# Attention's mask products: features in two 32-bit parts instead of three bfloat16 parts, masks in 32 bits

## The chip, the cores and the metric

The kernel runs on one core of one Trainium2 chip. The metric is the device time of one execution in microseconds; times of several executions are given by their median. The core's engines are called PE (TensorE), DVE (VectorE), ACT (ScalarE), POOL (GpSimd) and SP (SyncE, which issues most DMAs); PEld is PE's loading of weights.

## The reference

Four graph layers run one after the other on x (4096 nodes, 64 features) and one dense matrix adj (4096 x 4096, float32); each ends in a residual sum and a layer norm. Layer 0 is a Chebyshev filter (three products with adj), layer 2 a product with weights that decay along each row's non-zeros, layer 3 a hyperbolic aggregation over all pairs of nodes. The change is in layer 1:

```python
A_node = node_adj - jnp.diag(d_node)          # both are adj
node_support = concat([(A_node > 0) @ h, (A_node < 0) @ h], axis=1)
edge_output = gru_cell(node_support, h, w_ih_e, w_hh_e, b_ih_e, b_hh_e)
hw = h @ W
h_plus, h_minus = (A > 0) @ hw, (A < 0) @ hw
e_plus  = leaky_relu(concat([h_plus, h_minus]) @ a)
e_minus = leaky_relu(concat([h_minus, h_plus]) @ a)
att = softmax(where(A > 0, e_plus, where(A < 0, e_minus, -9e15)), axis=1)
edge_support = (att * A) @ hw
node_output = gru_cell(edge_support, h, w_ih_n, w_hh_n, b_ih_n, b_hh_n)
out = d_edge[:, None] * edge_output + d_node[:, None] * node_output
```

The score of a row does not depend on the column, so all that is needed of adj is the product of the positive (and negative) mask with h, the number of entries, and the product of adj itself with h. Here adj has no negative entry, and the kernel takes at run time the branch that has the positive mask alone (`signed` is false).

## The kernel before

**Stages.** The matrix is cut into 8 x 8 chunks of 512 x 512 floats (1 MB), held as 128 partitions x 4 blocks x 512. The first stage (to some 380 us) loads each chunk, turns it on PE, stores the turned one as `adj_t` and begins the Chebyshev filter; two further passes over parts of `adj_t` end it at about 568 us. Attention (568 to 841 us), the decay layer (to some 1150 us) and the hyperbolic layer follow. The order of the work is written out in Python loops, with steps of earlier rows put between the chunks; a scheduler then sets each engine's order by it, where `in_order` does not fix it.

**Attention.** The function `attention` goes through 64 chunks: rows g from 7 down to 0, in each the chunks c from 0 to 7. For a chunk, `masks` loads it (`load1`, L476, four tiles `at` of 1 MB), makes the mask `pos` (`positives`, L481, on DVE: 1 where the entry is over 0, in fp8, five tiles), and stores this mask for the decay layer (`keep_mask`, L778, issued by POOL). On the diagonal chunk (c = g) the diagonal is then set to zero (L1028), and `pos` is made a second time. `masks` runs two chunks ahead (`lead = 2`). Of the first three chunks, loaded early, `pos` is made before the branch.

PE then has three groups for a chunk, each over its four blocks of 128 rows, with 512 columns:

- `wide` (L1045): the mask with `sp_two`, the high and the middle bfloat16 part of the features side by side, 128 columns of weights;
- `narrow` (L1053): the mask with `sp_lo`, the low bfloat16 part, 64 columns, in two halves of the array by turns;
- `weighed` (L1062): adj itself with the features in float32, 64 columns, in two halves of the array by turns.

An even chunk has them in this order, an odd one in the opposite order, and chunk 7 has `narrow`, `wide`, `weighed`. The parts come from `split` (L244 to L248, five DVE operations for 512 nodes), called in `normed_third` behind layer 0's norm, seven times in the last pass over `adj_t` and once at the start of attention. The last column of the features is replaced: 1 in `sp_hi`, 0 in the others, so that the products also count the entries.

**A row's end and the steps put between.** After chunk 7 ACT copies the sums out of PSUM (`p_t` L1107, `a_t` L1110), and `group_end` gives six steps, one behind each of the next row's chunks. Behind chunk 0: the edge gates on PE (L840, L847), two tanh on ACT (`rz`, L856, with a table load ahead), DVE work, a tanh (`n`, L884), the scores and their exponentials on ACT (L911, L912), the `share` on DVE (L930). Behind chunk 1: a product with `a_t` (L937), its scaling by `share` on ACT (`gin`, L946), and the first half of the node gates (L840), which take the PSUM tile that `gin` has read. Behind chunk 2: the node's tanh (`rz` L874, `n` L884), the second half of the node gates, and the layer norm (a second table load and `ln_s`, L269), whose result is `nat_b`. Behind chunks 4 and 5: three bfloat16 parts of `nat_b` for the decay layer, and copies of them to other partitions, issued by POOL (`over_two`, `over_lo`, L988). In DVE's queue the `pos` of chunk 5 stands behind this layer norm. SP's queue holds the chunk loads and, in rows 7 to 4, reads of stored masks among them (L789 to L792).

Other tiles that the change moves: `part` (layer 0), `nat_b` and `nat_c` (later layers) have tiles of their own; `tr_o` lies in `sp_two`.

Of the kernel before, what the change touches and what calls it, by code (L numbers as in the profile page):

```python
# [8 lines left out]

F32 = mybir.dt.float32  # L10
BF16 = mybir.dt.bfloat16
U16 = mybir.dt.uint16
# [49 lines left out]
def gnn4_kernel(  # L62
# [21 lines left out]
    nc = tc.nc  # L84
# [85 lines left out]

    sp_two = keep.tile([P, NB, 2 * F], BF16, name="sp_two")
    sp_hi = sp_two[:, :, 0:F]
    sp_mid = sp_two[:, :, F : 2 * F]
    sp_lo = keep.tile([P, NB, F], BF16, name="sp_lo")

# [13 lines left out]
    def constant_fills():  # L189
        nc.gpsimd.memset(tr_a[F:P, :], 0.0)  # L190
        nc.gpsimd.memset(sp_hi[:, :, F - 1], 1.0)
        nc.gpsimd.memset(sp_mid[:, :, F - 1], 0.0)
        nc.gpsimd.memset(sp_lo[:, :, F - 1], 0.0)
        nc.gpsimd.memset(none_t, 0.0)
# [283 lines left out]

    def positives(pool, at, **more):
        pos = pool.tile([P, CB, GW], MASK, name="pos", **more)  # L480
        in_order(nc.vector.tensor_scalar(pos, at, 0.0, None, ALU.is_gt, saturate=False))  # L481
        return pos
# [26 lines left out]
    with tc.tile_pool(name="acc", bufs=1) as acc_p, tc.tile_pool(  # L509
# [212 lines left out]
        for g in reversed(range(NG - 1)):  # L722
# [42 lines left out]
    nat_c = three.tile([P, NB, F], F32, name="nat_c")  # L765

    tr_c = tr_x
    tr_o = sp_two[:, 0 : NB // 2, :]  # L770
    nat_b = three.tile([P, NB, F], F32, name="nat_b")
    middle = ctx.enter_context(ExitStack())
# [236 lines left out]
    def attention(signed, cols_p, sg, tl, ps_a, ps_p):  # L1009

        Q = 2 if signed else 1

        def masks(g, c):
            if g == NG - 1 and c < len(with_at):
                at, pos = with_at[c], with_pos[c] if c < len(with_pos) else None
            else:
                at, pos = load1(cols_p, g, c), None
            if not signed and pos is None:
                pos = positives(sg, at)
            mask = pos  # L1020
            if signed:
                mask = sg.tile([P, CB, GW], MASK, name="mask")
                in_order(nc.vector.tensor_scalar(mask, at, 0.0, None, ALU.not_equal, saturate=False))
            keep_mask(mask, g, c)
            if c == g:

                for k in range(CB):
                    in_order(nc.vector.tensor_tensor(at[:, k, cols(k)], at[:, k, cols(k)], not_ident, ALU.mult))  # L1028
                pos = None
            if pos is None:  # L1030
                pos = positives(sg, at)
            if not signed:
                return (pos,), (at,)
            neg = sg.tile([P, CB, GW], MASK, name="neg")
            up = sg.tile([P, CB, GW], F32, name="up")
            in_order(nc.vector.tensor_scalar(neg, at, 0.0, None, ALU.is_lt, saturate=False))
            nc.scalar.activation(up, at, AF.Relu)
# [3 lines left out]
        def wide(ps, two, c):  # L1041
            for k in range(CB):
                jb = c * CB + k
                for q in range(Q):
                    in_order(nc.tensor.matmul(  # L1045
                        ps[q], lhsT=sp_two[:, jb, :], rhs=two[q][:, k, :], start=(jb == 0), stop=(jb == NB - 1)
                    ))

        def narrow(ps, two, c):

            for q in range(Q):
                for k in range(CB):
                    in_order(nc.tensor.matmul(  # L1053
                        ps[q][k % 2 * F : k % 2 * F + F, :], lhsT=sp_lo[:, c * CB + k, :], rhs=two[q][:, k, :],
                        start=False, stop=False, skip_group_check=True,
                    ))

        def weighed(ps, parts, c):

            for k in range(CB):  # L1060
                for q in range(2) if signed else (k % 2,):
                    in_order(nc.tensor.matmul(  # L1062
                        ps[q * F : (q + 1) * F, :], lhsT=nat_a[:, c * CB + k, 0:F],
                        rhs=parts[q if signed else 0][:, k, :],
                        start=(c == 0 and k < 3 - Q), stop=(c == NCH - 1 and k >= CB - 3 + Q), skip_group_check=True,
# [10 lines left out]
        lead = 0 if signed else 2  # L1076
        ahead = [masks(*order[n]) for n in range(lead)]
        steps = [nothing, nothing, lambda ps_p: put_ones(last_row), lambda ps_p: turn_pairs(ps_p, last_row)]
        for n, (g, c) in enumerate(order):
            if n == 0:  # L1080
                normed_third(last_row, sum_last[mine(last_row), :], ps_p)
            if n + lead < len(order):
                ahead.append(masks(*order[n + lead]))
# [3 lines left out]
            two, parts = ahead.pop(0)  # L1087
# [29 lines left out]
    for signed in (False, True):  # L1117
        with cmp.Else() if signed else tc.If(all_positive > 0) as block:
            cmp = block
            with tc.tile_pool(name="cols1", bufs=4 if not signed else 2) as cols_p, tc.tile_pool(name="sign1", bufs=1 if signed else 5) as sg, tc.tile_pool(  # L1120
                name="tail1", bufs=1
# [5 lines left out]
    front.close()  # L1127


    inside = const.tile([P, NB], F32, name="inside")  # L1130
# [600 lines left out]
```

## Time and profile before

| what | us |
|---|---|
| median of three executions | 1499.1 |
| lowest and highest | 1495.8 and 1501.7 |
| span of the profiled execution (first to last instruction) | 1490.4 |
| PE busy | 1355.1 (91%) |
| DVE busy | 1026.1 (69%) |
| ACT busy | 753.2 (51%) |
| POOL busy | 122.7 (8%) |

For the profiled execution the profile gives the span alone; what lies around it is seen only in the distance of 8.7 us between the span and the median of the executions.

A row of the groups reads: line, engine, operation, output<-inputs by the program's names, shapes and types, number; then busy time in us and the mean of one in ns; then the idle time of the engine ahead of it and what ended that. Matmuls overlap and their ends are modelled, so the distance from start to start says what one costs. A float32 product appears as two records. In the order of time a line gives start, time taken, engine, line, operation, number, and in brackets the idle time ahead of it.

### The profile page before, as it was taken

To read this page: it belongs to the slowest core of one execution; us is meant where nothing else is said; L and a number is where in the kernel's file an instruction comes from. 1 tells how busy PE (TensorE), PEld (TensorE's weight loads), DVE (VectorE), ACT (ScalarE), POOL (GpSimd) and SP (SyncE) were. 2 spreads that over 40 slices of the span, in tenths; PEclk is the share of its full clock that TensorE was granted. 3 is DMA by queue.
4 is the path that set the end of the run, shared out by engine and by line. 5 is a ranking of instruction groups with operands and counts; after the bars stand their busy time and mean duration, and the time that the engine had idled before them with its cause. 6 is when DMAs were issued, how large, how long until landed. Compare 5 with 4: busy or idle time off the path is not lost.

```text
span 1490.4 us, 19538 instructions
## 1 busy us (share of the span) xinstructions
PE 1355.1 (91%) x7124; PEld 609.0 (41%) x7124; DVE 1026.1 (69%) x2004; ACT 753.2 (51%) x1303; POOL 122.7 (8%) x206
## 2 busy tenths in 40 slices
PE   5999999999999989889999899999788899889884
PEld 3555555565344323333333332333333334334343
DVE  5989998886000467666677422435899999999995
ACT  3554444342000110222222277564789999999993
POOL 4101100000000002222222100000000000000000
PEclk8999999999999999999999999999899999999996
DMA  9999999997588799788988555552534453544430
GB/s 290 413 410 410 411 410 402 388 359 306 202 281 294 299 419 344 288 307 314 333 328 324 199 176 173 164 168 93 198 141 170 153 216 144 206 165 173 149 113 11
DMA packets 103362, 385.40 MB, mean 259 GB/s; under 512 B 16341, under 2 KB 17369, under 8 KB 71257
## 3 DMA queue, kind: packets, MB, share of 16 engines
q1 hardware_dynamic: 84256, 296.78, 55.2%
q0 software_dynamic: 15616, 85.73, 14.0%
q10 hardware_dynamic: 3384, 1.56, 0.4%
q8 instruction: 58, 0.95, 0.3%
q14 instruction: 48, 0.39, 0.1%
HBM read 297.26 MB, written 85.20 MB: 257 GB/s over the span
## 4 chain that ended last, share of the span: by engine, by line
PE 51%; DVE 20%; ACT 16%; issue 6%; DMA 5%; ACTq 1%; POOL 0%; SPq 0%; DVEq 0%; POOLq 0%
PE tp L637 7%; PE pass L545 7%; PE w_ps L545 7%; PE cnt_ps L1319 4%; PE acc_ps L1275 4%; PE pass L538 3%; PE h_ps L538 3%; PE post L556 2%; DVE at_m L1486 2%; ACT w L1637 2%; DMA at<-adj_t 2%; DVE f L1647 2%; ACT w L1448 2%; ACT rt L1638 2%; ACT wt L1324 2%
## 5 line engine op out<-in xcount | busy, mean ns | idle before, releaser
L644 ACT COPY at<-tp 128x512 f32<-128x512 f32 x256 | 132.6, 598 | 132.2 <-issue 91.9
L1324 ACT ACTIVATE wt<-cnt_ps 128x512 uint16<-128x512 f32 x208 | 115.6, 595 | 70.6 <-PE cnt_ps L1319 65.7
L637 PE MATMUL tp<-ident,raw 128*128 128x128 f32 x1024 | 133.1, 284 | 14.6 <-DMA raw<-in_adj_dram 9.9
L670 DVE TENSOR_REDUCE dpart<-raw 128x4 f32<-128x2048 f32 x64 | 145.4, 2272 | 0.5 <-DMA raw<-in_adj_dram 0.4
L672 DVE TENSOR_REDUCE lows<-raw 128x1 f32<-128x2048 f32 x64 | 145.3, 2271 | 0.0
L1500 PE MATMUL sums_ps<-at_d,nat_c 128*64 128x512 f32 x288 | 140.6, 607 | 2.4 <-DVE at_d L1479 1.8
L637 PEld LDWEIGHTS tp<-ident,raw 128*128 128x128 f32 x1024 | 116.5, 144 | 53.8 <-issue 30.9
L1062 PE MATMUL a_ps<-at,nat_a 128*64 128x512 f32 x512 | 122.4, 605 | 2.9 <-DVE at L1028 2.9
L481 DVE TENSOR_SCALAR pos<-at 128x2048 fp8e4<-128x2048 f32 x72 | 87.6, 1231 | 48.4 <-DMA at<-adj_t 47.9
L1512 PE MATMUL sums_ps<-at_m,nat_c 128*64 128x512 f32 x224 | 107.3, 600 | 0.0
L545 PE MATMUL w_ps<-at,cheb_n 128*128 128x512 f32 x224 | 101.1, 595 | 0.0
L545 PE MATMUL pass<-at,cheb_n 128*128 128x512 f32 x224 | 100.0, 604 | 0.7 <-DVE cheb_n L698 0.7
L1439 PE MATMUL v_ps<-rv,tr_a 64*128 64x512 f32 (+1 forms) x288 | 79.4, 629 | 22.6 <-DVE rt L1662 22.4
L1319 PE MATMUL cnt_ps<-m,follow 128*64 128x512 fp8e4 x480 | 81.7, 391 | 4.6 <-ACT wt L1324 2.1
L1662 DVE SCALAR_TENSOR_TENSOR rt<-v_ps,rt 128x1024 f32<-128x1024 f32 x72 | 83.1, 1154 | 3.7 <-ACT rt L1638 3.4
L1647 DVE SCALAR_TENSOR_TENSOR f<-rt,w 128x1024 f32<-128x1024 f32 x72 | 82.6, 1154 | 2.2 <-ACT rt L1673 2.1
L1650 DVE TENSOR_TENSOR at_d<-at_d,f 128x1024 f32<-128x1024 f32 x72 | 82.9, 1151 | 0.1
L1326 DVE TENSOR_SCALAR wt<-cnt_ps 128x512 uint16<-128x512 f32 x48 | 33.2, 692 | 66.6 <-PE cnt_ps L1319 66.6
L1673 ACT ACTIVATE rt<-rt 128x1024 f32<-128x1024 f32 x72 | 72.4, 1005 | 9.5 <-DVE rt L1662 9.2
L1486 DVE TENSOR_TENSOR at_m<-post,at_m 128x512 f32<-128x512 f32 x112 | 74.4, 678 | 4.0 <-PE post L1484 3.9
L1484 PE MATMUL post<-ident,f 128*128 128x128 f32 x448 | 69.6, 285 | 7.4 <-DVE at_m L1486 6.4
L1637 ACT ACTIVATE w<-w 128x1024 f32<-128x1024 f32 x72 | 72.0, 1002 | 5.0 <-DVE w L1466 5.0
(394 smaller groups left out, 2214.4 us busy)
## 6 DMA issues: line engine op xcount, KB each, us to landing
at<-adj_t SPq DMA_DIRECT2D x122, 1024.0 KB, 6.8
raw<-in_adj_dram SPq DMA_DIRECT2D x64, 1024.0 KB, 12.9
adj_t<-at POOLq DMA_DIRECT2D x64, 1024.0 KB, 8.0
at_d<-adj_t SPq DMA_DIRECT2D x36, 1024.0 KB, 4.7
at_m<-adj_t SPq DMA_DIRECT2D x28, 1024.0 KB, 6.9
mask_t<-pos POOLq DMA_DIRECT2D x64, 256.0 KB, 5.7
m<-mask_t SPq DMA_DIRECT2D x120, 128.0 KB, 2.8
m<-mask_t SPq DMA_DIRECT2D x60, 256.0 KB, 3.8
```

Of the source, the lines that this page charges most:

```text
L545: in_order(nc.tensor.matmul(ps, lhsT=cheb_n[:, jb, k : k + 2, :], rhs=rhs, start=first, stop=last))
L637: in_order(nc.tensor.transpose(tp[:, cols(b)], raw[:, b, cols(k)], ident))
L644: nc.scalar.copy(at[:, k, :], tp)
L670: in_order(nc.vector.tensor_reduce(dpart[:, g, c, :], raw, AX.X, ALU.add))
L672: in_order(nc.vector.tensor_reduce(lows[:, n : n + 1], raw.rearrange("p b j -> p (b j)"), AX.X, ALU.min))
L1062: in_order(nc.tensor.matmul(ps[q * F : (q + 1) * F, :], lhsT=nat_a[:, c * CB + k, 0:F], rhs=parts[q if signed else 0][:, k, :], start=(c = ...
L1319: in_order(nc.tensor.matmul(cnt[a][r * HP : (r + 1) * HP, :], lhsT=follow, rhs=chunks[c][odd][2 * a + r][:, k, :], start=(h == 2 * NB - 1) ...
L1324: in_order(nc.scalar.activation(wt[odd][a], cnt[a], AF.Relu, scale=-128.0))
L1486: work.append(lambda to=to, tp=tp: nc.vector.tensor_tensor(to, tp, to, ALU.mult))
L1500: in_order(nc.tensor.matmul(bank[0:F, :], lhsT=nat_c[:, j * CB + k, :], rhs=own[t][:, k, :], start=(i == j and k == 0), stop=(j == seq[-1] ...
L1512: in_order(nc.tensor.matmul(bank[F:P, :], lhsT=nat_c[:, above * GB + k, :], rhs=mirrored[tm][:, k, :], start=(k == 0 and above == seq[0]), ...
L1647: nc.vector.scalar_tensor_tensor(f, rts.pop(m)[:, :, cm], T_MAX, ws.pop(m)[:, :, cm], ALU.min, ALU.mult)
```

## The change

[...] The stored mask stays fp8, but is now made by ACT from the chunk itself (the function Sign, 64 times 128 x 2048, two tiles), before the diagonal is set to zero; so `positives` runs once for each chunk, also on the diagonal. Only the first chunk's `pos` is made before the branch. To make room, `part`, `nat_b`, `nat_c` and `tr_o` move into parts of other tiles. An even chunk and chunk 7 have `wide`, `weighed`; the other odd chunks `weighed`, `wide`.

```diff
-    sp_two = keep.tile([P, NB, 2 * F], BF16, name="sp_two")
-    sp_hi = sp_two[:, :, 0:F]
-    sp_mid = sp_two[:, :, F : 2 * F]
-    sp_lo = keep.tile([P, NB, F], BF16, name="sp_lo")
+    def parts_tile(name):
+        return keep.tile([P, NB, 2 * F], F32, name=name, tag="parts")
+
+    before = parts_tile("before")
+    now = {}
...
-        nc.gpsimd.memset(sp_hi[:, :, F - 1], 1.0)
-        nc.gpsimd.memset(sp_mid[:, :, F - 1], 0.0)
-        nc.gpsimd.memset(sp_lo[:, :, F - 1], 0.0)
...
+    def split_two(src, two):
+
+        w = src.shape[2]
+        high, rest = two[:, :, 0:w], two[:, :, F : F + w]
+        nc.vector.tensor_copy(high.bitcast(F32R), src)
+        nc.vector.tensor_tensor(rest.bitcast(F32R), src, high, ALU.subtract)
...
-    def positives(pool, at, **more):
-        pos = pool.tile([P, CB, GW], MASK, name="pos", **more)
-        in_order(nc.vector.tensor_scalar(pos, at, 0.0, None, ALU.is_gt, saturate=False))
+    def positives(pos, at):
+        in_order(nc.vector.tensor_scalar(pos.bitcast(F32R), at, 0.0, None, ALU.is_gt))
         return pos
...
-        split(g, nat_a[:, gs, 0:F], F - 1, sp_hi, sp_mid, sp_lo)
+        split_two(nat_a[:, gs, 0 : F - 1], now["parts"][:, gs, :])
...
-        part = acc_p.tile([P, NB, F], F32, name="part")
+        part = before.rearrange("p b f -> p (b f)")[:, 0 : N // 2].rearrange("p (b f) -> p b f", b=NB)
...
+        now["parts"] = parts = parts_tile("parts")
+        nc.gpsimd.memset(parts[:, :, F - 1 : F], 1.0)
+        nc.gpsimd.memset(parts[:, :, 2 * F - 1 : 2 * F], 0.0)
...
-        with_pos = [positives(ahead_p, at, bufs=3) for at in with_at[:1]]
+        first_pos = positives(ahead_p.tile([P, CB, GW], F32, name="first_pos"), with_at[0])
         for work in due:
             work[2]()
-        with_pos += [positives(ahead_p, at, bufs=3) for at in with_at[1:]]
...
-    nat_b = three.tile([P, NB, F], F32, name="nat_b")
+    nat_b = tr_a[:, N // 2 : N].rearrange("p (b f) -> p b f", b=NB)
...
+        if not signed:
+            ring = [first_pos] + [sg.tile([P, CB, GW], F32, name=f"pos{q}") for q in range(2)]
+
+        def masks(n):
+            g, c = order[n]
+            at = with_at[n] if n < len(with_at) else load1(cols_p, g, c)
+            mask = sg.tile([P, CB, GW], MASK, name="mask", bufs=1 if signed else 2)
+            if signed:
...
+            else:
+                nc.scalar.activation(mask, at, AF.Sign, saturate=False)
+                pos = ring[n % 3]
             keep_mask(mask, g, c)
             if c == g:
                 for k in range(CB):
                     in_order(nc.vector.tensor_tensor(at[:, k, cols(k)], at[:, k, cols(k)], not_ident, ALU.mult))
-                pos = None
-            if pos is None:
-                pos = positives(sg, at)
+            if n:
+                positives(pos, at)
...
                     in_order(nc.tensor.matmul(
-                        ps[q], lhsT=sp_two[:, jb, :], rhs=two[q][:, k, :], start=(jb == 0), stop=(jb == NB - 1)
+                        ps[q], lhsT=parts[:, jb, :].bitcast(F32R), rhs=two[q][:, k, :].bitcast(F32R),
+                        start=(jb == 0), stop=(jb == NB - 1),
                     ))
...
             work = [
                 lambda: wide(wide_ps, two, c),
-                lambda: narrow(wide_ps, two, c),
-                lambda: weighed(a_ps, parts, c),
+                lambda: weighed(a_ps, of, c),
             ]
-            if c == NCH - 1:
-                work = [work[1], work[0], work[2]]
-            elif c % 2:
+            if c % 2 and c < NCH - 1:
                 work.reverse()
...
+    some = parts_tile("some").rearrange("p b f -> p (b f)")
+    nat_c = some[:, N // 2 : N].rearrange("p (b f) -> p b f", b=NB)
+    tr_o = some[:, 0 : N // 4].bitcast(BF16).rearrange("p (m n) -> p m n", n=P)
```

More of the change, by code (lines that the diff above doesn't have):

```diff
@@ L10 @@
 F32 = mybir.dt.float32
+F32R = mybir.dt.float32r
 BF16 = mybir.dt.bfloat16
@@ L756, in gnn4_kernel @@
         with_at = [load1(pool, NG - 1, c, "raw") for c, pool in enumerate((staying_p, staying_p, front_p))]
-        with_pos = [positives(ahead_p, at, bufs=3) for at in with_at[:1]]
+        first_pos = positives(ahead_p.tile([P, CB, GW], F32, name="first_pos"), with_at[0])
         for work in due:
             work[2]()
-        with_pos += [positives(ahead_p, at, bufs=3) for at in with_at[1:]]
     going.close()
     three = ctx.enter_context(tc.tile_pool(name="three", bufs=1))
-    nat_c = three.tile([P, NB, F], F32, name="nat_c")
     tr_c = tr_x
-    tr_o = sp_two[:, 0 : NB // 2, :]
-    nat_b = three.tile([P, NB, F], F32, name="nat_b")
+    nat_b = tr_a[:, N // 2 : N].rearrange("p (b f) -> p b f", b=NB)
     middle = ctx.enter_context(ExitStack())
@@ L1011, in attention @@
         Q = 2 if signed else 1
-        def masks(g, c):
-            if g == NG - 1 and c < len(with_at):
-                at, pos = with_at[c], with_pos[c] if c < len(with_pos) else None
-            else:
-                at, pos = load1(cols_p, g, c), None
-            if not signed and pos is None:
-                pos = positives(sg, at)
[L1020 to L1023, printed above, removed]
+        if not signed:
[5 more added lines that the diff above has]
+            if signed:
+                in_order(nc.vector.tensor_scalar(mask, at, 0.0, None, ALU.not_equal, saturate=False))
+                pos = sg.tile([P, CB, GW], F32, name="pos") if n else first_pos
+            else:
+                nc.scalar.activation(mask, at, AF.Sign, saturate=False)
+                pos = ring[n % 3]
             keep_mask(mask, g, c)
@@ L1028, in masks @@
                     in_order(nc.vector.tensor_tensor(at[:, k, cols(k)], at[:, k, cols(k)], not_ident, ALU.mult))
-                pos = None
-            if pos is None:
-                pos = positives(sg, at)
+            if n:
+                positives(pos, at)
             if not signed:
                 return (pos,), (at,)
-            neg = sg.tile([P, CB, GW], MASK, name="neg")
+            neg = sg.tile([P, CB, GW], F32, name="neg")
             up = sg.tile([P, CB, GW], F32, name="up")
-            in_order(nc.vector.tensor_scalar(neg, at, 0.0, None, ALU.is_lt, saturate=False))
+            in_order(nc.vector.tensor_scalar(neg.bitcast(F32R), at, 0.0, None, ALU.is_lt))
             nc.scalar.activation(up, at, AF.Relu)
@@ L1045, in wide, with weighed @@
                     in_order(nc.tensor.matmul(
-                        ps[q], lhsT=sp_two[:, jb, :], rhs=two[q][:, k, :], start=(jb == 0), stop=(jb == NB - 1)
-                    ))
[L1049 to L1058, printed above, removed]
+                        ps[q], lhsT=parts[:, jb, :].bitcast(F32R), rhs=two[q][:, k, :].bitcast(F32R),
+                        start=(jb == 0), stop=(jb == NB - 1),
+                    ))
+        def weighed(ps, of, c):
             for k in range(CB):
@@ L1063, in weighed @@
                         ps[q * F : (q + 1) * F, :], lhsT=nat_a[:, c * CB + k, 0:F],
-                        rhs=parts[q if signed else 0][:, k, :],
+                        rhs=of[q if signed else 0][:, k, :],
                         start=(c == 0 and k < 3 - Q), stop=(c == NCH - 1 and k >= CB - 3 + Q), skip_group_check=True,
@@ L1076, in attention @@
         lead = 0 if signed else 2
-        ahead = [masks(*order[n]) for n in range(lead)]
+        ahead = [masks(n) for n in range(lead)]
         steps = [nothing, nothing, lambda ps_p: put_ones(last_row), lambda ps_p: turn_pairs(ps_p, last_row)]
@@ L1082, in attention @@
             if n + lead < len(order):
-                ahead.append(masks(*order[n + lead]))
+                ahead.append(masks(n + lead))
             if c == 0:
@@ L1086, in attention @@
                 a_ps = ps_a.tile([P, GW], F32, name="a_ps")
-            two, parts = ahead.pop(0)
+            two, of = ahead.pop(0)
             work = [
                 lambda: wide(wide_ps, two, c),
-                lambda: narrow(wide_ps, two, c),
-                lambda: weighed(a_ps, parts, c),
-            ]
-            if c == NCH - 1:
-                work = [work[1], work[0], work[2]]
-            elif c % 2:
+                lambda: weighed(a_ps, of, c),
+            ]
+            if c % 2 and c < NCH - 1:
                 work.reverse()
@@ L1119, in gnn4_kernel @@
             cmp = block
-            with tc.tile_pool(name="cols1", bufs=4 if not signed else 2) as cols_p, tc.tile_pool(name="sign1", bufs=1 if signed else 5) as sg, tc.tile_pool(
+            with tc.tile_pool(name="cols1", bufs=4 if not signed else 2) as cols_p, tc.tile_pool(name="sign1", bufs=1) as sg, tc.tile_pool(
                 name="tail1", bufs=1
```

## The prediction

> **What bounds the kernel now.** I read the page first (TensorE, PE, is busy 91% of the span), then the table by stage, then the attention stage's waits and order of time. The change acts between 568 and 841 us, where eight rows of eight chunks are worked through in about 34 us each. Two rows of that stage (length, then busy time of PE, weight loads, DVE, ACT, POOL, the granted clock, the DMA share, GB/s):
>
> ```profile
> 740.00:774.00 34.00, 31.82 (x164) 12.24 (x160) 24.37 (x73) 8.12 (x17) 10.74 (x16) 1.00 0.87 322
> 774.00:808.00 34.00, 31.85 (x163) 12.35 (x162) 25.10 (x75) 8.17 (x18) 8.95 (x13) 1.00 0.86 318
> ```
>
> PE bounds a row (31.8 of 34 us). DMA is close behind: 0.87 x 34 = 29.6 us. DVE has 9 us free and ACT 26. Who waits in the stage:
>
> ```profile
> DVE pos L481 <- DMA at<-adj_t: 47.9, 15, 6.5
> ...
> PE post L840 <- ACT gin L946: 11.3, 7, 2.8
> ...
> PE p_ps L1053 <- DVE pos L481: 6.4, 7, 1.3
> ```
>
> PE stops twice in each row with group work, seven rows: for ACT's `gin` (1.6 us on average) and for a `pos` that DVE makes late, behind the layer norm (0.9 us). DVE waits 3.2 us at a time for loads, but two chunks ahead, so nobody pays for that. PE's time of two chunks, and two float32 groups of the first stage as a measure:
>
> ```profile
> 653.34 0.60 PE L1053 MATMUL p_ps<-pos,sp_lo 128*64 128x512 fp8e4 x4
> 653.87 1.90 PE L1045 MATMUL p_ps<-pos,sp_two 128*128 128x512 fp8e4 x8
> 655.70 0.62 PE L1053 MATMUL p_ps<-pos,sp_lo 128*64 128x512 fp8e4 x4
> 656.16 1.88 PE L1062 MATMUL a_ps<-at,nat_a 128*64 128x512 f32 x8
> ...
> 302.44 1.98 PE L637 MATMUL tp<-ident,raw 128*128 128x128 f32 x16
> 304.25 3.60 PE L545 MATMUL w_ps<-at,cheb_n 128*128 128x512 f32 x8
> 307.69 1.98 PE L637 MATMUL tp<-ident,raw 128*128 128x128 f32 x16
> ```
>
> **Removed from PE: the narrow products.** From start to start, `narrow` takes 0.53 and 0.46 us in two chunks, eight wide products 1.83 (0.229 each), a chunk's `weighed` some 1.78. Without `narrow` a change between wide and float32 products remains; where one shows (wide 703.90, weighed 704.87) four wide take 0.97, against 0.92. So 0.99 less 0.10 goes for two chunks: 0.445 a chunk, 3.56 a row, 28.5 us in all, if a wide product costs what it did.
>
> **Does it?** No row shows a product of this 32-bit type. [...]
>
> **DVE.** `pos` becomes 32 bits wide. Above: a rate half as fast, some 2.3 us (a 128x2048 TENSOR_REDUCE takes 2.27). Nearest rows: the float32 copy of the same size, and today's `pos`, which converts as well:
>
> ```profile
> 19.89 1.23 DVE L664 COPY cheb_n<-nat_a 128x2048 f32<-128x2048 f32 x1
> ...
> L481 DVE TENSOR_SCALAR pos<-at x72: 1211/1220/1623, 567.6 to 836.2; 128x2048 fp8e4<-128x2048 f32 x72
> ```
>
> I take 1.22, no change; 72 become 64, so DVE gains 10 us that nobody waits for. `split` goes from five operations to two (1.7 us to some 0.8, eight times): seven lie in pass 3, where the loads at 414 GB/s set the pace, the last before a PE that is busy. Nothing for the end. The three POOL memsets at the start stand beside other POOL work before the first load lands; the two new ones fall where POOL is idle. The tiles that move (`part`, `nat_b`, `nat_c`, `tr_o`) bring no instruction. Zero for these.
>
> **Added to ACT: 64 Sign operations for the stored mask.** The nearest rows, by shape:
>
> ```profile
> L1637 ACT ACTIVATE w<-w 128x1024 f32<-128x1024 f32 x64 | 67.2, 1049 | 5.0 <-DVE w L1466 5.0
> ...
> L1637 ACT ACTIVATE w<-w 128x512 f32<-128x512 f32 x8 | 5.0, 620 | 0.0
> ```
>
> That is 0.838 ns an element, and 1.049 + 0.858 = 1.91 us for 2048 (twice the 1024 row, 2.10, is the most). That is 15.3 us a row on an ACT with 26 free: as a sum it fits. But ACT works in order, and the order of the changed program puts a Sign before the table load of the gates, one before the `n` tanh, one before `gin`, one before the node's `rz`, one before the second table load. ACT's gaps there, in a row of before:
>
> ```profile
> 779.06 1.28 ACT L856 ACT_TABLE_LOAD   x1 [4.19 <-PE post L847]
> 780.35 0.66 ACT L856 ACTIVATE rz<-post 128x256 f32<-128x256 f32 x2
> 782.09 0.42 ACT L884 ACTIVATE n<-n 128x256 f32<-128x256 f32 x1 [1.07 <-DVE share L897]
> ...
> 785.59 1.36 ACT L946 ACTIVATE gin<-post,share 128x192 f32<-128x192 f32 x4 [2.29 <-DVE share L930]
> ...
> 787.78 0.42 ACT L874 ACTIVATE rz<-gin 128x256 f32<-128x256 f32 x1 [0.84 <-DVE gin L870]
> ...
> 797.02 0.20 ACT L269 ACTIVATE ln_s<-ln_ve 128x4 f32<-128x4 f32 x1 [2.56 <-DVE ln_ve L264]
> ```
>
> With its chunk landed in time, a Sign costs what sticks out of the gap: 1.91 - 1.07 = 0.84 before `n`, none before `gin` (2.29), 1.07 before `rz` (0.84), none before `ln_s` (2.56). Late, it costs more. DVE's `pos` of the chunk whose Sign stands before the first table load waited until 779.63 for its load; a Sign then ends at 781.54, and the table load begins 2.5 us after 779.06. Also, the mask has two tiles where `pos` had five, and its write lands 5.7 us after issue (median): 5.7 + 1.9 = 7.6 us for two chunks, 30 us a row, hardly under PE's new 28.2.
>
> **What is late next.** Behind ACT's steps wait `node_gates` on PE, and on DVE, behind the whole layer norm, the fifth chunk's `pos`. PE reaches the first stop 0.45 us earlier and the second 0.90 earlier (two narrow steps lie between). First wait: + 0.45 + chain, the chain between 0.84 (landed) and 2.5 + 0.84 = 3.3 (late); I take 2.0, near the middle, because of 15 load waits over seven such rows, two a row, one at this place. Second: + 0.90 + 1.07, up to 1.9 more if the Sign before the second table load is late; I take none, because the longer first wait gives the loads time. Row: -3.56 + 2.45 + 1.97 = +0.86; seven rows +6.0. The first row has no group work, and from 571 to 596 us a DMA share of 0.93; its gain is at most 0.07 x 25 = 1.7 us, and its last chunk, the diagonal, is corrected only after the seventh Sign: I take +2. Sum **+8 us**. Ends: all landed, -0.30 x 7 - 1.7 = -4; all late, (-3.56 + 3.75 + 3.87) x 7 + 4 = +32, of which I keep +20, since a row that lasts longer lands its loads sooner. Loads wait for the Sign too, but need the later `weighed` anyway; SP's mask reads in four rows stand before loads and wait for masks some 0.7 us later: within the range. The span would be 1498; the runs' median lies 8.7 us above it, which I carry over: 1499 + 8 = **1507**.
>
> **Rivals.**
> 1. ACT absorbs the Signs: loads land early, since nothing else moves. For it: 26 us free a row. Against: the order above. Only the earlier arrival at both stops stays: -3.56 + 1.35 = -2.2 a row, seven rows -15.5, about 1483, faster. DMA's 29.6 us allows it. It decides where the Sign before the first table load starts within the 4.19 us gap.
> [...]
> 3. `pos` at half rate: DVE 24.4 + 8 x 1.05 = 33 us a row; with its waits it is the bound, some +20, 1519.
> [...]
>
> **How the numbers follow.** Main case 0.55 (1495 to 1519), rival 1 0.22, rival 2 0.18, rival 3 0.05. A measurement tells 0.5%, 7.5 us, from no change. The main case centres on that border: same 0.25, slower 0.30. Faster: 0.22; slower: 0.30 + 0.18 + 0.05 = 0.53. The range leaves out the outer half of rival 1 and of rival 2: 1481 to 1533.
>
> **What would show it.** Right: `narrow` gone, wide at 0.215 to 0.23 apart, ACT near 23 us a row, PE's waits for `gin` near 4 us and for the fifth `pos` near 3, rows of about 34 to 35 us. Wrong: wide spaced 0.43 (rival 2), `pos` over 2 us (rival 3), rows under 32.5 with the `gin` wait under 2.5 (rival 1), or a difference outside 568 to 841 us.

## The result: 2.6% slower, and the profile after

The changed kernel takes 1537.4 us (median of 4, 1531.7 to 1545.7) against 1497.5 for the kernel before in the same comparison: ratio 1.0263, 95% interval 1.0223 to 1.0303. The forecast was 1507 with a range up to 1533. The direction holds, the size does not: +40 us in place of +8. The profiled execution has a span of 1530.0 us (1490.4 before) and took 1531.7 us itself. In every execution whose span is on record the time lies 1.7 to 2.7 us above the span; so most of the 8.7 us that the forecast carried over from span to median was only that the profiled execution of the kernel before was a short one.

The page of the changed kernel, its first part and two of its groups (busy us, mean ns of one; then idle time before them):

```profile
PE 1365.5 (89%) x6868; PEld 624.3 (41%) x6868; DVE 1011.5 (66%) x1972; ACT 868.7 (57%) x1367; POOL 118.0 (8%) x205
...
L1029 ACT ACTIVATE mask<-at 128x2048 fp8e4<-128x2048 f32 x64 | 121.8, 1908 | 73.6 <-DMA at<-adj_t 33.1
...
L1060 PE MATMUL a_ps<-at,nat_a 128*64 128x512 f32 x512 | 137.3, 667 | 3.4 <-DVE at L1035 3.4
```

In the changed kernel `wide` multiplies both parts of the features, kept side by side in the tile `parts` in the program's type `float32r`, at once, 128 columns as before; `narrow` is gone, and `pos`, in the same type, has a ring of three tiles. PE has 256 products fewer and is busy 10 us longer (1355.1 before). The weighed products of L1060, which the change does not touch, take 137.3 us; before it was 122.4. Something slowed PE's own work. The table by stage, two rows of the attention stage, each from its edge gates to the next (the columns are those of the prediction's first fence):

```profile
685.43:723.83 38.40, 32.15 (x131) 14.15 (x129) 22.90 (x70) 22.22 (x25) 8.26 (x11) 0.91 0.76 280
763.96:801.22 37.26, 32.49 (x131) 14.36 (x129) 23.91 (x75) 22.37 (x26) 7.95 (x12) 0.91 0.79 288
```

These rows take 37 to 38 us instead of 34 (the seven with group work lie between 35.6 and 44.8). PE is busy about as long as before, 32 us, with some 30 instructions fewer, and the granted clock is 0.91 where it was 1.00. ACT is at 22.3 us, near the 23 of the forecast. DMA share has fallen from 0.87 to below 0.80, so loads are not the limit by amount. Who waits in the stage (total us, times, longest):

```profile
ACT mask L1029 <- DMA at<-adj_t: 33.1, 18, 2.9
...
ACT mask L1029 <- DMA mask_t<-mask: 26.5, 13, 5.3
...
PE post L845 <- ACT gin L951: 21.0, 7, 6.0
...
PE p_ps L1051 <- DVE pos L486: 18.0, 7, 3.2
```

PE stops at the two places that the prediction named. The wait for `gin` has grown from 11.3 to 21.0 us, that for `pos` from 6.4 to 18.0. Sign waits for its load and for one of the two mask tiles. What follows a stop is seen in PE's order of time, one row of the changed kernel:

```profile
736.10 0.98 PE L845 MATMUL post<-whh_n,tr_a 64*128 64x256 f32 x4 [4.10 <-ACT gin L951]
737.01 2.07 PE L1051 MATMUL p_ps<-pos,parts 128*128 128x512 f32 x4
739.01 2.31 PE L1060 MATMUL a_ps<-at,nat_a 128*64 128x512 f32 x8
...
743.75 1.20 PE L1051 MATMUL p_ps<-pos,parts 128*128 128x512 f32 x4
744.79 1.09 PE L1051 MATMUL p_ps<-first_pos,parts 128*128 128x512 f32 x4
745.81 3.65 PE L1060 MATMUL a_ps<-at,nat_a 128*64 128x512 f32 x16
```

Four wide products take 2.07 us behind the stop of 4.10 and 1.20 (1.04 from start to start) seven us later. The first are at half pace. The granted clock (third number from the end) is half for 3.42 us, from 0.3 us after PE resumed:

```profile
732.00:736.39 4.39, 0.29 (x2) 0.29 (x4) 3.23 (x13) 4.25 (x9) 1.21 (x2) 1.00 0.80 321
736.39:739.81 3.42, 3.42 (x10) 1.46 (x10) 2.48 (x5) 2.50 (x3) 0.96 (x2) 0.50 0.21 83
739.81:743.20 3.39, 3.39 (x18) 1.07 (x16) 0.75 (x3) 0.42 (x1) 0.00 (x0) 1.00 0.48 150
```

At full pace eight wide products need 745.81 - 743.75 = 2.06 us from start to start, 0.2575 each on average, against 0.229 before.

From such records I split PE's time in the stage, from the first wide product to the first count product, into idle time over 0.25 us (**stops**), what groups of wide and weighed products take beyond their steady pace where they exceed it by 12% (**slow**; the steady pace is 0.236 us a wide product in bfloat16, 0.262 in 32 bits, with its share of the changes between products, 0.2255 a weighed record), and the pace that is left:

| us | stage | stops | slow | wide | narrow | weighed | group steps |
|---|---|---|---|---|---|---|---|
| before | 273.3 | 23.4 | 2.5 | 59.6 | 32.9 | 114.6 | 40.3 |
| changed | 306.1 | 51.5 | 26.6 | 68.2 | 0 | 118.0 | 41.8 |
| difference | +32.8 | +28.1 | +24.1 | +8.6 | -32.9 | +3.4 | +1.5 |

Of the 39.6 us between the spans, 32.8 lie in the stage; 2.4 lie ahead of it and 4.3 behind.

### The profile page after: what moved, and what is told of

Its sections match the earlier page's. It is cut to its first block, busy times and chain, and to the rows that moved or that the text cites. A ratio compares the mean times of both kernels' runs of the same rounds, so it can differ in the third digit from the quotient of the medians.

```text
span 1530.0 us, 19134 instructions
## 1 busy us (share of the span) xinstructions
PE 1365.5 (89%) x6868; PEld 624.3 (41%) x6868; DVE 1011.5 (66%) x1972; ACT 868.7 (57%) x1367; POOL 118.0 (8%) x205
## 3 DMA queue, kind: packets, MB, share of 16 engines
q0 software_dynamic: 15616, 85.73, 13.8%
## 4 chain that ended last, share of the span: by engine, by line
PE 50%; ACT 16%; DVE 14%; issue 9%; DMA 9%; POOL 1%; ACTq 0%; SPq 0%; POOLq 0%; DVEq 0%
PE pass L550 6%; PE w_ps L550 6%; PE tp L642 6%; DMA raw<-in_adj_dram 4%; PE cnt_ps L1317 4%; PE pass L543 4%; PE acc_ps L1273 3%; PE a_ps L1060 3%; PE h_ps L543 3%; DVE at_m L1484 2%; PE post L561 2%; ACT w L1635 2%; DMA at<-adj_t 2%; ACT wt L1322 2%; DVE rt L1660 2%
## 5 line engine op out<-in xcount | busy, mean ns | idle before, releaser
L1029 ACT ACTIVATE mask<-at 128x2048 fp8e4<-128x2048 f32 x64 | 121.8, 1908 | 73.6 <-DMA at<-adj_t 33.1
L1498 PE MATMUL sums_ps<-at_d,some 128*64 128x512 f32 x288 | 143.9, 620 | 2.0 <-DVE at_d L1477 1.8
L642 PE MATMUL tp<-ident,raw 128*128 128x128 f32 x1024 | 132.0, 282 | 15.2 <-POOL state_hhn L386 6.7
L1060 PE MATMUL a_ps<-at,nat_a 128*64 128x512 f32 x512 | 137.3, 667 | 3.4 <-DVE at L1035 3.4
L1510 PE MATMUL sums_ps<-at_m,some 128*64 128x512 f32 x224 | 110.2, 615 | 0.0
L543 PE MATMUL h_ps<-at,cheb_n 128*64 128x512 f32 x288 | 75.4, 610 | 0.0
```

What stands on the lines that cost most here:

```text
L543: in_order(nc.tensor.matmul(ps[q * F : (q + 1) * F, :], lhsT=cheb_n[:, jb, k, :], rhs=rhs, start=first, stop=last, skip_group_check=True,))
L642: in_order(nc.tensor.transpose(tp[:, cols(b)], raw[:, b, cols(k)], ident))
L1029: nc.scalar.activation(mask, at, AF.Sign, saturate=False)
L1060: in_order(nc.tensor.matmul(ps[q * F : (q + 1) * F, :], lhsT=nat_a[:, c * CB + k, 0:F], rhs=of[q if signed else 0][:, k, :], start=(c == 0 ...
L1498: in_order(nc.tensor.matmul(bank[0:F, :], lhsT=nat_c[:, j * CB + k, :], rhs=own[t][:, k, :], start=(i == j and k == 0), stop=(j == seq[-1] ...
```

## The experiments

All medians in us; the ratio is to the kernel before in the same comparison (its medians lay between 1497.5 and 1499.6). "Stage", "stops" and "slow" are those of the table above, from one profiled execution each; products of zero weights (the runs with "fill") are counted with the weighed ones. The executions of one kernel lie 2 to 22 us apart, so a difference of a few us in these three columns shows nothing by itself.

| run | median | ratio, 95% interval | stage | stops | slow |
|---|---|---|---|---|---|
| before_no_narrow | 1491.1 | 0.9956 (0.9938 to 0.9975) | 271.1 | 36.1 | 15.2 |
| no_narrow_fill | 1485.4 | 0.9914 (0.9893 to 0.9935) | 264.7 | 23.8 | 8.2 |
| before_split | 1500.5 | 1.0014 (0.9994 to 1.0035) | 279.4 | 25.8 | 5.5 |
| before_sign | 1533.8 | 1.0233 (1.0195 to 1.0271) | 315.2 | 49.3 | 15.1 |
| tiny_dve | 1512.1 | 1.0085 (1.0058 to 1.0112) | 280.6 | 36.8 | 15.4 |
| tiny_act | 1519.0 | 1.0106 (1.0052 to 1.0160) | 289.8 | 41.2 | 18.8 |
| tiny_chain | 1538.8 | 1.0269 (1.0194 to 1.0344) | 304.4 | 48.0 | 28.2 |
| tiles6 | 1531.7 | 1.0226 (1.0188 to 1.0265) | 307.4 | 55.7 | 23.2 |
| ring6 | 1525.4 | 1.0186 (1.0151 to 1.0221) | 296.0 | 48.0 | 19.7 |
| split6 | 1523.7 | 1.0192 (1.0146 to 1.0238) | 295.2 | 49.1 | 20.2 |
| mid6 | 1535.9 | 1.0267 (1.0230 to 1.0303) | 309.6 | 55.5 | 26.6 |
| mid6_split | 1529.6 | 1.0221 (1.0189 to 1.0254) | 298.1 | 52.4 | 20.1 |
| ring6_mid_split | 1528.4 | 1.0206 (1.0165 to 1.0246) | 302.4 | 55.6 | 21.3 |
| fill | 1539.0 | 1.0280 (1.0242 to 1.0318) | 313.8 | 43.4 | 14.6 |
| ring6_fill | 1525.4 | 1.0181 (1.0163 to 1.0199) | 300.0 | 37.8 | 15.0 |
| mask_dve | 1546.0 | 1.0295 (1.0249 to 1.0340) | 325.0 | 62.0 | 33.0 |
| late2 | 1559.0 | 1.0387 (1.0342 to 1.0433) | 333.9 | 80.1 | 23.4 |
| mask_dma | 1567.8 | 1.0457 (1.0416 to 1.0499) | 340.1 | 82.7 | 24.9 |

### Is it Sign? tiny_act, tiny_dve

The theory was that Sign, in ACT's queue ahead of `gin` and `rz`, costs the time, by waiting or by its length; the rival, that the 32-bit products do.

```diff
-    nc.scalar.activation(mask, at, AF.Sign, saturate=False)
+    mask = stored[n % 2]                       # two tiles, set to 1.0 once
+    nc.scalar.activation(mask[:, :, 0:1], at[:, :, 0:1], AF.Sign, ...)          # tiny_act
+    in_order(nc.vector.tensor_scalar(mask[:, :, 0:1], at[:, :, 0:1], 0.0, None, ALU.is_gt, ...))  # tiny_dve
```

> Left out: the stored mask's values (two constant tiles are stored); ACT's Sign is kept at its place for one column of four blocks only, so it still waits for the chunk's load and for a mask tile, but takes about 0.2 us instead of 1.9. Queue theory (what costs is that each Sign, at its early place, holds ACT until a load has landed or a mask tile is free): most of the loss stays, 1510 to 1535 us. Length theory (what costs is the 1.9 us that each Sign adds in front of gin and rz): nearly all goes, 1475 to 1490. Rival, products theory (the 32-bit products and the three-tile pos ring cost the time, ACT does not): no change, 1530 to 1540.

> Left out: the stored mask's values, as in the run with the short Sign; here nothing at all stands on ACT, and DVE marks the tile with 128x4 elements just ahead of pos, so that the stores keep their pace. Queue and length theory alike: before's 1497, less 28.5 for the narrow products, plus 256 x 0.03 = 8 for a dearer wide product: about 1477, 1470 to 1490. Products theory: above 1515, with PE's waits for pos still 2 to 3 us long.

By its number tiny_act lies in the range of the queue theory; tiny_dve lies in no range. With nothing on ACT the kernel is still 12.5 us slower than before (ratio 1.0085), where both Sign theories said 20 us faster. Sign accounts for 25 of the 40 us: 18 go when it is short; whether the 7 more of tiny_dve are real is not shown, since the two intervals overlap. (tiny_dve is not free of waits: DVE's mark waits 29.4 us for a mask tile to be stored.) The waits of tiny_act speak against the queue theory:

```profile
ACT mask L1033 <- DMA mask_t<-mask: 74.8, 28, 6.4
ACT mask L1033 <- DMA at<-adj_t: 70.8, 31, 6.3
...
PE post L845 <- ACT gin L951: 23.3, 7, 5.6
...
PE p_ps L1055 <- DVE pos L486: 9.5, 7, 1.7
```

The short Sign, at the same place, waits 145.6 us for these two where the long one waited 59.6, and the time falls all the same. PE's wait for `gin` stays (23.3 us, 21.0 in the changed kernel); what falls is the wait for `pos`, from 18.0 to 9.5. So the 18 us go with Sign's length, not with its waiting in ACT's queue. More than Sign was missing in my sum, and it could not yet be said what.

### One part alone: before_no_narrow, before_sign

```diff
 # before_no_narrow
-    lambda: narrow(wide_ps, two, c),
 # before_sign
+    mask = sg.tile([P, CB, GW], MASK, name="mask", bufs=...)     # two where no entry is negative
+    nc.scalar.activation(mask, at, AF.Sign, saturate=False)     # pos keeps three tiles
```

> The kernel before without its narrow products (left out: the third, lowest part of the features in the mask products); no Sign, 8-bit masks, bfloat16 products, five pos tiles. Steady pace theory (PE's time falls by what the rows of narrow say): -32.9 us in the stage, about 1467. Arrival theory (PE reaches the waits for gin and for the fifth pos 1.35 us a row earlier and stands there instead, and the longer stops cost clock): -32.9 + 9 of stops + 12 of clock = -12, about 1486. Products theory (the 32-bit products are what made the changed kernel slow even with nothing on ACT, 1512): 1465 to 1475.

> The kernel before with one thing added: the stored mask is made by ACT's Sign into two tiles of its own, and pos keeps three tiles instead of five, as in the changed kernel; products unchanged. If Sign is a charge of its own, as the 25 us between the changed kernel (1537) and the one with DVE's short mark (1512) say: 1515 to 1530. If it costs only because PE got ahead of ACT by the narrow products' time: 1500 to 1510.

Removing 32.9 us of PE work brings 6.6 us, and 2.2 in the stage. This is the run that settles most. The waits of that kernel in the stage:

```profile
PE p_ps L1045 <- DVE pos L481: 17.5, 10, 2.9
PE post L840 <- ACT gin L946: 14.1, 7, 3.2
```

Stops rise by 12.7 us and slow products by 12.7; dearer changes between products take 5.2 more (wide 60.8, weighed 118.6). The arrival theory said 9 + 12. Rival 1 of the prediction, -15.5 us, is a sum for such a kernel, in which no Sign delays ACT: it counted 9.5 us of longer stops and nothing for slowed products. No Sign and no 32-bit product is in this kernel. From here, tiny_dve adds 32-bit products (and the ring of three `pos` tiles and DVE's mark, which no run takes apart), and its stage differs by 9.5 us: wide 69.4 instead of 60.8, stops +0.7, slow +0.2. The products theory is therefore right about 8.6 us, the wide products' own price; the two traces show no more. (The rest of the 21 us between their medians lies mostly ahead of the stage, which begins at 577.2 us there against 567.5; between 567.5 and 577.2 it moves from kernel to kernel, and I have no cause for that.)

Sign, put on the kernel before, costs 36 us. It is a charge of its own, larger than either branch of the expectation (the three `pos` tiles in place of five come with it; no run has them alone):

```profile
ACT mask L1022 <- DMA mask_t<-mask: 48.6, 21, 5.1
ACT mask L1022 <- DMA at<-adj_t: 43.0, 20, 5.7
PE p_ps L1054 <- DVE pos L481: 26.0, 7, 9.3
```

### Does the lost clock cost time? fill, no_narrow_fill, ring6_fill

Products of zero weights are put on PE ahead of the two stops, adding zero to the running sum.

```diff
+    for q in range(2):
+        in_order(nc.tensor.matmul(a_ps[q * F : (q + 1) * F, :], lhsT=wq[:, 1, 0:F],
+            rhs=nat_a.rearrange("p b f -> p (b f)")[:, 0:GW], start=False, stop=False, ...))
```

> The changed kernel with eight more float32 products of zero weights a row, from the second row on, half of them just ahead of the first node gates and half ahead of the fifth chunk's wide products, where PE stands for 3.0 and 2.6 us on average; they add zero and take some 1.8 us at each place. Clock theory (short stops let the granted clock fall to half, worth 25 us of slower products): 1512 to 1522. Rival (the slow stretches come from the 32-bit products and have nothing to do with the stops): 1537 or up to 10 us more.

> The kernel without narrow products (1491; left out: the lowest of three parts) with two float32 products of zero weights (0.9 us together) ahead of the first node gates and two ahead of the fifth chunk's wide products of each row from the second on; it stands there 2.0 and 2.2 us on average, and no Sign or tile ring disturbs the row. Clock theory (the half clock after these stops, 12 us of slower products, is part of the chain): the clock stays, 1480 to 1486. Rival (the slow products are absorbed by the next stop, so the clock lost costs nothing): 1489 to 1496.

> The changed kernel with six mask tiles and six loaded tiles (1525) with two such products ahead of the first node gates and four ahead of the fifth chunk's wide products; nothing left out. Clock theory: 17 us of the slow products go, part of them on the path, 1510 to 1518. Rival: 1523 to 1535, as with fill on the changed kernel itself, where the stops shortened but the wait for gin came later.

In the changed kernel the slow products fell by 12 us and the time did not move (1539.0). By itself that spoke for the rival, but the time from the edge gates to the node gates had grown there from 75.1 to 90.1 us over seven rows, with Sign waiting for loads and mask tiles in that stretch. Without Sign the answer is clearer: 28 products more, and 1485.4 instead of 1491.1. The clock theory had said 1480 to 1486. The two medians are from different comparisons; their intervals just do not overlap. The same place in both kernels, in the row that begins at some 705 us, first without, then with fill (L1102):

```profile
713.13 0.70 PE L840 MATMUL post<-whh_n,tr_a 64*128 64x256 f32 x4 [1.89 <-ACT gin L946]
713.77 1.42 PE L1045 MATMUL p_ps<-pos,sp_two 128*128 128x512 fp8e4 x4
715.11 3.20 PE L1062 MATMUL a_ps<-at,nat_a 128*64 128x512 f32 x8
```

```profile
712.28 1.08 PE L1102 MATMUL a_ps<-nat_a,wq 128*64 128x512 f32 x4
714.24 0.70 PE L842 MATMUL post<-whh_n,tr_a 64*128 64x256 f32 x4 [0.88 <-ACT gin L950]
714.87 1.04 PE L1049 MATMUL p_ps<-pos,sp_two 128*128 128x512 fp8e4 x4
715.84 1.94 PE L1066 MATMUL a_ps<-at,nat_a 128*64 128x512 f32 x8
```

Behind the filled stop the wide products take 1.04 us instead of 1.42, the weighed ones 1.94 instead of 3.20. (In the next row 2.24 us of the stop are left, and the wide products take 1.89 us with fill as without.) In the stage slow falls by 7.0 us, the stops by 12.3, and the weighed and zero products take 12.7 more; the stage gets 6.4 shorter. So the lost clock is on the path: the second half of the node gates stands behind these slow products, and ACT, DVE and the late `pos` behind it. ring6_fill brought nothing over ring6 (1525.4 both), as its rival had said. But with Sign in the row more products were put in, eight a row in fill and six in ring6_fill against four here, and the weighed and zero products took some 26 and 18 us more while the stops fell by 8.1 and 10.2. Whether other waits take the place of what the clock gives there, or these products' own time does, stays open; Sign with four a row was not run.

### What moves the stops: before_split, split6

The node gates are issued one chunk later.

```diff
-    [of(1, shared)], [of(0, node_gates)], [of(0, node_sum)],
+    [of(1, shared)],
+], [
+    [of(0, node_gates)], [of(0, node_sum)],
...
-] + norm, [[nothing]], [[decay_parts]], ...
+] + norm, [[decay_parts]], ...
```

> The kernel before with nothing but the node gates one chunk later. Its stops for gin were 11.3 us, with 2 us of clock behind them: 1484 to 1490 if they go, 1495 to 1500 if the stop only moves to the pos that DVE makes late.

> The changed kernel with six mask tiles and the node gates issued one chunk later (step list cut in two ahead of them, the empty step left out), so that ACT's gin has 3.3 us more. Stop theory (PE stands for gin, 21 us, and loses clock after it): 1507 to 1520. Loop theory (a row is 38 to 40 us by loads, Sign and tiles whatever PE does): 1528 to 1535.

On the kernel before: nothing (1500.5). On the changed one with six mask tiles: 8 us by the medians, with intervals that overlap, and less than the stop theory said. The waits of split6 show why:

```profile
PE p_ps L1059 <- DVE pos L486: 30.5, 6, 7.5
PE p_ps L1059 <- DVE first_pos L486: 12.9, 3, 6.2
```

The wait for `gin` is gone, and the 20.9 us of it (in tiles6) turn up at `pos`, which waited 21.4 there and waits 43.4 here. PE passes the first place sooner and stands at the second.

### Which of Sign's waits? tiles6, ring6, mid6, mid6_split, ring6_mid_split, tiny_chain

```diff
 # tiles6: four more mask tiles in with_at[2], idle after the third chunk
+    stored += [spare[:, q * CB * GW : (q + 1) * CB * GW]... for q in range(4)]
 # ring6: besides, two more tiles for the loaded chunks
+    held = [cols_p.tile(...) for q in range(4)] + with_at[:2]
 # mid6, mid6_split, ring6_mid_split: Sign of chunk n + 1 in the step of chunk n
+    sign(n + 1, ahead[1][1][0])
 # tiny_chain: tiny_act, but short only for c in (3, 4, 5)
```

> The changed kernel with six mask tiles instead of two (the four others lie in the third chunk's tile of the first row, which nothing uses after that chunk). Ring theory (ACT's 37 us of waiting for a mask tile to be stored, 26.5 by name and 10.5 without one, stand in front of gin and rz): 1512 to 1525. Queue theory without the ring (waits for loads and the 1.9 us themselves): 1530 to 1540.

> The changed kernel with six mask tiles (1532) and six tiles for the loaded chunks instead of four, the two more being the first row's tiles, which nothing uses until the last row; Sign at its early place. Load theory (a load is issued only when a tile comes free four chunks on, 5 to 9 us before ACT's Sign wants it, and ACT's steps wait behind): waits of Sign for loads from 47 to under 15 us, 1505 to 1520. Length theory (Sign's 1.9 us in the chain): 1525 to 1532.

> The changed kernel with six mask tiles (1532 by itself) and Sign of a chunk issued one chunk later, when its load has landed for pos, but a chunk before its weighed products, so that the loaded tile is not held longer; the diagonal chunk's Sign stays. Load theory (in ACT's queue Sign waits for its load, and ACT's steps wait with it): 1510 to 1520, near the 1512 of the kernel with DVE's short mark. Length theory (the 1.9 us themselves): 1528 to 1535. Rival, loop theory (the loads come late because tiles are freed late, whoever waits for them): above 1535, as with Sign two chunks later (1559).

> Both: six mask tiles, Sign one chunk later, node gates one chunk later. Stop and load theory together: PE bounds the row again, 30 to 32 us, 1475 to 1495. Loop theory: 1525 or more.

> The last one with Sign one chunk later and the node gates one chunk later. Load theory: 1490 to 1510, as PE then bounds the row. Chain theory (edge gates to the fifth chunk's pos is a chain of ACT and DVE steps whose length neither PE's work nor the loads set): 1515 to 1530.

> Left out: part of the stored mask's values. The kernel with the short Sign at ACT (1519), but short only for the fourth to sixth chunk of each row, whose Signs stand among ACT's steps for gin, rz and the layer norm; the five others take their 1.9 us (two fixed tiles as in the short ones). Place theory (1.9 us costs only where ACT's group steps stand behind it): 1519 to 1525. Amount theory (each Sign costs its share of the 18 us wherever it stands): 1519 + 5/8 x 18 = 1530.

By the medians six mask tiles bring 6 us and six loaded tiles 6 more. Neither step is clear of the noise; both together are, just (ring6's interval ends at 1.0221, the changed kernel's begins at 1.0223), and ring6 lies in the range of the length theory. A later Sign brings nothing, nor does it on top of either. In tiny_chain the three Signs inside ACT's steps are short and the time does not move (1526 to 1548, the widest of all runs), while eight short ones bring 18. So place alone is refuted, and the parts do not add up. Sign's price as a whole is shown (25 us on the changed kernel, 36 on the one before), and tiny_act shows that much of it goes with its length; a full split into length, load wait and tile wait, and which of the eight Signs of a row counts, is not shown.

### Can Sign's work go elsewhere? mask_dve, late2, mask_dma

```diff
 # mask_dve
-    nc.scalar.activation(mask, at, AF.Sign, saturate=False)
+    in_order(nc.vector.tensor_scalar(mask, at, 0.0, None, ALU.is_gt, saturate=False))
 # late2: Sign of chunk n behind chunk n's own products
 # mask_dma: mask_t is written from the 32-bit pos, converted on the way
+    keep_mask(pos, g, c)
```

> Nothing left out: the stored mask is made by DVE (1.2 us a chunk, in 8-bit), ahead of pos, instead of ACT's Sign. DVE's row then grows from about 24.5 to 24.5 + 8 x 1.23 = 34.3 us, over PE's 30 to 31, and loads are waited for on DVE. Queue and length theory: DVE becomes the bound, rows of 34.5 to 36 us, 1500 to 1520. Products theory: later than the changed kernel, above 1540, since DVE's pos is what PE waits for and this delays it.

> Nothing left out: Sign of a chunk is issued two chunks later, behind that chunk's own products, when its load has long landed (the diagonal chunk's stays where it is). ACT does the same work, without waits for loads. Queue theory: most of the loss goes, 1480 to 1500, PE's wait for gin near 2 us. Length theory: half stays, 1505 to 1520, gin waits near 4 us. Products theory: no change, 1530 to 1540.

> Nothing left out: the stored mask is written straight out of the 32-bit pos by a transfer that converts to 8 bits; ACT keeps only the eight diagonal chunks' Signs. Sign theory: ACT and DVE are then as in the kernel with DVE's short mark, 1505 to 1515, if the transfers cost no more than before. Rival: the transfer reads four times the bytes (5 MB a row more, some 16 us of DMA time at 320 GB/s on 29.6 of 34): loads come late, 1540 or more.

None is faster than the change itself; late2 and mask_dma are clearly slower, mask_dve by the medians alone (the intervals overlap). With mask_dve, rows of 38 to 46 us: DVE has 1.22 us a chunk more, waits for mask tiles itself (16.7 us by name), and what stands behind it is later. In late2 stops come to 80 us; by the order of the program a loaded tile is then held until its Sign is done and the next load starts later, but I did not test that by itself. In mask_dma the rival was right, as the stage's row shows:

```profile
573.00:914.00 341.00, 257.49 (x997) 113.20 (x998) 175.26 (x525) 73.83 (x132) 57.58 (x95) 0.89 0.97 248
```

DMA is busy 0.97 at 248 GB/s: fewer bytes a second at a fuller queue.

Two versions beat both kernels, before_no_narrow by 0.44% and no_narrow_fill by 0.86% of the time before; both leave out the lowest of the three parts of the features.

## Why the prediction was wrong

The sum for the stage was -28.5 (narrow) + 36.5 (stops: seven rows of 4.42, and 5.6 in the first row, to end at +2 there) = +8. By the same terms the trace has:

- **Narrow: right.** -28.5 forecast with the changes between products; -32.9 + 3.4 = -29.5 measured, -27.7 in before_no_narrow.
- **The stops: right in place, a little too large.** +36.5 forecast, +28.1 measured. The wait for `gin` was to be near 4 us and is 3.0 on average (21.0 / 7), the fifth `pos` near 3 and is 2.6 to 3.0 in six rows. By terms: +9.7 for `gin` where 17.2 were counted (2.45 x 7), +11.6 for `pos` where 13.8 were (1.97 x 7), +6.8 elsewhere where the first row had 5.6. Sign takes 1.91 us, as forecast.
- **What a stop does to the products behind it: the failed step.** "Row: -3.56 + 2.45 + 1.97" counts the time that PE stands and nothing after it. Behind 12 of the 14 stops of the seven rows (two in each, 1.8 to 6 us long) the clock falls, and the products behind lose 1.4 to 2.2 us each time; with those of the first row they take 24.1 us more than before. In PE's account this term is as large as the whole miss (24.8 us in the stage): the others, stops -8.4, wide +8.6, narrow and changes -1.0, group steps +1.5, nearly cancel. That the lost clock costs time is shown without Sign (no_narrow_fill, just clear of the noise); on the changed kernel it is not, since fill took 12 us of slow products away, put more products in, and the time did not move. The trace of before had it in view: the stop of 2.75 us at 606.8 us was followed by four wide products in 1.74 us instead of 0.97. Because most of its stops were of 0.8 to 1.8 us, the clock of its rows was 1.00, and I carried that pace over to rows whose stops I had myself made twice as long.
- **A wide product at 0.229 us: too low.** That a 32-bit product keeps the bfloat16 pace, as the forecast counted by taking nothing for it, no run shows; it was my estimate. The runs show one record, not two as for a float32 product (0.860 us, 3.44 / 4 in the row at 304.25 us of before), and rival 2's 0.43 is out; but it starts 0.2575 us after the one before, on average over a group of eight: 8.6 us more in the table. I took the first stage's transposes, which load 128 float32 columns each and start 0.113 us apart, for proof that a 32-bit load hides. They do not show it: the records of their loads (L637 of before) are 140 ns long (median), and those of the wide products' loads longer. The records of the loads, before and after (shortest, median, longest ns):

```profile
L1045 PEld LDWEIGHTS <-sp_two x256: 95/98/152, 568.1 to 839.1; 128*128 128x128 bf16 x128
```

```profile
L1051 PEld LDWEIGHTS p_ps<-pos,parts x168: 186/188/338, 577.7 to 869.8; 128*128 128x128 f32 x168
```

  These loads' records are 188 ns long (median) instead of 98. Standing bare ahead of each wide product, they would come to 256 x 0.188 = 48 us, an estimate from these records; the table shows 8.6 more, so most of a load still lies beside a product.

- **`pos`: right.** 1.22 us, so rival 3 is out:

```profile
L486 DVE TENSOR_SCALAR pos<-at x42: 1193/1223/1557, 571.5 to 867.8; 128x2048 fp32r<-128x2048 f32 x42
```

- **Outside the stage: zero forecast, 6.7 us measured,** 2.4 ahead and 4.3 behind. Profiled executions of kernels with bfloat16 products have 647.9 to 651.6 us behind the stage, those with 32-bit parts 650.1 to 653.1. I did not find the cause.
- **The mechanism of Sign: right at the first stop in three rows of seven, and there one step longer than I wrote.** PE waits 1.8 to 1.95 us for `gin` in four rows, 3.55, 4.10 and 5.97 in three. In the four, edge gates to node gates take 9.2 to 9.3 us against 9.0: a Sign whose load has landed in time costs this chain 0.2 to 0.3 us, not the 0.84 that the prediction took, and the rest of the longer wait is PE's earlier arrival, as rival 1 had it. ACT's order of time in the last and longest of the three, a row of 44.8 us (start, length, the wait before it):

```profile
839.60 1.91 ACT L1029 ACTIVATE mask<-at 128x2048 fp8e4<-128x2048 f32 x1 [2.58 <-DMA at<-adj_t]
841.53 1.28 ACT L861 ACT_TABLE_LOAD   x1
...
848.99 1.91 ACT L1029 ACTIVATE mask<-at 128x2048 fp8e4<-128x2048 f32 x1 [2.92 <-issue]
850.81 1.34 ACT L951 ACTIVATE gin<-post,share 128x192 f32<-128x192 f32 x4
```

  The late Sign ahead of the table load is the one that the prediction priced at up to 2.5 us. The Sign ahead of `gin` I had put at nothing, in a gap of 2.29 us; it starts after a wait of 2.92 us of its own, for which the trace names no releaser, and `gin` begins at 850.81 us. With before's gap of 2.29 us after ACT's last step, which ended at 846.07, it would have been 848.36.

Why did a saving of 33 us on the busiest engine bring 6.6? In each row the time from the edge gates to the node gates is 9.0 us (median) in the kernel before and 9.0 without narrow; from there to the end of the second stop it is 13.6 and 14.8; only the rest, 11.2 and 10.4, got shorter. The first two thirds of a row are a chain through ACT, DVE and short PE steps, slowed further by the half clock. The prediction's "PE bounds a row" is thus wrong for this part: PE was busy 93% of a row and still did not set its length there, and the narrow products filled stops that now stand open.

## What to carry to other kernels

Before taking work off a busy engine, cut the row at its stops and ask for each piece whether the engine or the chain behind the stop sets its end; only the pieces without a stop get shorter. Price a longer stop on TensorE with what comes after it: here 28 us more of stops came with 24 us more in slowed products. Four products of zero weights a row, put into the stops, brought 5.7 us where taking 32.9 us of work off PE had brought 6.6; with Sign in the row, six or eight brought nothing. An operation with room by the sum (15 us on an engine with 26 free) can be dear when it stands in order ahead of a chain: kept at its place and with its waits, but short, it cost 18 us less.

## What the runs showed of the hardware

- **Stops of 1.6 to 2.8 us lose the clock too, one time in two.** In the attention stages of the twenty profiled executions, a stop over 0.25 and under 1.6 us was followed by a stretch of half clock before the next stop 15 times in 136, one of 1.6 to 2.8 us 61 times in 111, a longer one 114 times in 124. All these stretches of half clock are 3.41 us long, or two to four times that, and lie on one grid of 3.41 us in each execution. What goes with them is PE's idle share of the 3.41 us just ahead on that grid: where PE stood 60% of it or more, half clock followed 178 times in 178; where 50 to 60%, 48 times in 71; where less, 51 times in 1475. So the stretch can begin well after the stop: 1.7 us behind one of 1.81 us that ended at 618.6 us in the changed kernel, where it slowed only the weighed products of 620.4 us.
- **A wide product with 32-bit parts on both sides** is one record, 0.2575 us from start to start for 512 columns (on average over a group of eight), 12% above the bfloat16 one at 0.229, with weight loads of 188 ns instead of 98.
- **A transfer that converts 32 to 8 bits** takes 10.4 us (median) to land in mask_dma, where the same 256 KB unconverted take 4.6 in the changed kernel. But the queues are full beside it, share 0.97 at 248 GB/s, and the eight unconverted ones of the same run take 12.7. It also reads 1 MB where the other reads 256 KB; no run takes these apart.
